# One transpose for the last 16 columns of four batches, and copies inside SBUF for the row tiles

## The chip, the cores and the metric

The kernel runs on one core of a Trainium2 chip. The time is device microseconds for one execution. The core's engines are named as the profile names them: PE is TensorE (PEld its weight loads), DVE is VectorE, ACT is ScalarE, POOL is GpSimd, and SP is SyncE, which here only issues DMAs.

## What is computed

The input x has 32 batches of 128 tokens by 144 columns, with one condition vector of 144 per batch. Four layers follow one another: a transformer layer with normalised q and k (L0), a rotation of x inside a subspace of 64 columns (L1), a plain transformer layer (L2), and a transformer layer with four experts in place of its MLP (L3). All is float32. Cut to what the change touches:

```python
def _modulate(x, shift, scale):
    return x * (1.0 + scale) + shift

ada = jax.nn.silu(c) @ W_ada + b_ada
shift_msa, scale_msa, gate_msa, shift_mlp, scale_mlp, gate_mlp = jnp.split(ada, 6, axis=-1)
h = _modulate(_layernorm(x), shift_msa, scale_msa)
x = x + gate_msa * _attention(h, W_qkv, b_qkv, W_proj, b_proj)
h = _modulate(_layernorm(x), shift_mlp, scale_mlp)
mlp = jax.nn.gelu(h @ W_fc1 + b_fc1, approximate=True) @ W_fc2 + b_fc2
x = x + gate_mlp * mlp
```

L0 and L3 have the same frame; L3's MLP is `hmid = gelu(xf @ w1[e] + b1[e])` for four experts, weighted by a softmax over the two largest of four gate logits `xf @ w_gate`. The rotation is

```python
U, _ = jnp.linalg.qr(P)
R = _rotation(cond, W, b)                  # expm of a skew matrix, 64 x 64 per batch
z = jnp.einsum('btn,nd->btd', x, U)
x_rot = x + jnp.einsum('btd,nd->btn', jnp.einsum('btd,bde->bte', z, R) - z, U)
```

## The kernel before

x stays in SBUF with tokens on the partitions. A product that contracts over the 144 columns needs them on the partitions, of which there are 128. So each normalised batch h is split into a main part of 128 columns and a rest of 16, both transposed on PE: `hM` (128 x 128 per batch) and `hR` (the 16 columns; a 17th row of ones carries the bias of the weights). Each product is then a main product over 128 rows and a rest product added to it.

The rest product needs only 17 rows, fewer than a fourth of PE's 128. So the 16 columns are laid down four times before the transpose, at columns 0, 32, 64 and 96 of the tile `xr`; its transpose then holds four copies at partitions 0, 32, 64 and 96, in four *row tiles* of 32. Rest products of four different outputs use one row tile each (`rows4(m)`, 32 rows) and run on PE side by side, with the rest weights `wqkR`, `wvR`, `w1R` laid out to match. L0's q, k and v are formed differently (`by_token0`), with one rest product over all 128 rows, in which only 17 are filled.

The batches go in eight groups of four (G = 4). What a group goes through for one normalisation, of kind "a" (before attention) or "m" (before the MLP):

- `ln_stats` (L616): mean and variance on DVE, then on POOL the normalised main part `xh` (L636) and the four copies of the rest in `xr` (L638), per batch. `xr` comes from a ring of 7 zeroed tiles.
- `ln_T` (L645): per batch two transposes on PE, `xh` (L655) and `xr` (L656), into one PSUM bank, and two ACT instructions (L658) that scale and shift them, with `modM` and `modR`, into the group's `hM` and `hR`. `modR` holds shift and scale of the 16 columns four times over.
- The readers: `qk_chunks` (four products of 512 columns for q and k of a group: four main products, then four rest products, both in the helper `both`, L668), `values` by `by_token` (two batches at a time), `fc1` (three row tiles, up to three outputs at a time; for most calls the rest products stand first and the main products a gap later), and `gate_logits` (L1026), which multiplies the four batches into four column tiles.

The rotation has its own transposes: `rotate_T` (L988) turns main and rest of the four batches, eight transposes, and `rotate_in` (L1005) multiplies by U's main part `uM` and rest `uR`.

The order of all work is written out by hand. Time goes in *ticks*, one per batch and layer; in each tick the scores of one batch (two calls, n = 0 and 1) alternate with the weighing of another, and between them are named *gaps* ("a", "e", "t", "stats", "b0", "b", "den", "pre1", "c", "y1" ... "z", "d"), into which `put` places the other work. Each engine carries out its instructions in that order. The second and third attention layers start at ticks 35 and 67. With t0 the first tick of a group, in the second layer:

- the "a" statistics of batch i stand in tick t0 - 6 + i, its `ln_T` in gap "b" of the tick after (group 0: t0 - 4 + i // 2);
- `qk_chunks` in gap "c" of t0 - 2; the values at t0 and t0 + 1;
- the "m" statistics at t0 + 3 + i and its `ln_T` in gap "d" of the same tick; `fc1` at t0 + 8 and t0 + 9;
- the rotation of the next layer's input, `rotate_T`, `rotate_in` and `rotate`, in the ticks t0 - 8 and t0 - 7.

In the third layer `ln_T` of "a" stands in gap "d" of its statistics' own tick, and the gates at t0 + 7 are followed by `moe1` from t0 + 8 on. Gap "d" stands at a tick's end from tick 35 on, "b" and "c" in its middle. SP's queue holds the loads of x and the weights, of each group's gates (`load_gates`, L305), and the stores of the output (L1138).

## Time and profile before

| | us |
|---|---|
| median of 3 runs | 1312.52 (1311.24 to 1313.37) |
| profiled execution, its time | 1303.81 |
| profiled execution, span of its instructions | 1302.1 |

Groups of instructions that the change touches, by line, in the profiled execution:

| line | what | count | mean ns |
|---|---|---|---|
| L655 PE | transposes of xh, "a" and "m" | 96 + 96 | 286, 275 |
| L656 PE | transposes of xr, "a" and "m" | 96 + 96 | 281, 273 |
| L658 ACT | hR out of PSUM, "a" and "m" | 96 + 96 | 462, 461 |
| L638 POOL | xr, 128x64 | 187 | 420 |
| L668 PE | rest products of qk, 32x512 | 128 | 640 |
| L668 PE | rest products of fc1, 32x512 | 448 | 619, 613 |
| L1000 PE | transposes of the rotation's rest | 32 | 277 |
| L305 SP | loads of the gates | 48 | |

A matmul's duration is modelled, and matmuls overlap: the next begins long before the one before it ends, so that what an instruction takes of PE's time is read from the distance between starts. Most matmuls here count twice, as float32 takes two passes; a transpose counts once. L668 is a helper's line, so its groups are told apart by their tiles.

### The profile page before, as it was taken

The page shows a single profiled execution, that of the slowest core. Times are in us where ns is not written, and L with a number is a line of the kernel's source. Part 1 is how long each engine was busy: PE and PEld are TensorE (multiplying, and loading weights), DVE is VectorE, ACT ScalarE, POOL GpSimd, SP SyncE. Part 2 cuts the span into 40 slices and gives each one's busy share as a digit, 9 for nine tenths or more (in the row PEclk, how much of TensorE's full clock was granted, in tenths as well). Part 3 has the DMA queues.
Part 4 walks back from the last instruction along what each step waited for, and adds up shares of the span by engine and source line. Part 5 has one row for each costly group of instructions (what it writes and reads, how often), then busy time and mean ns, then how long its engine had stood idle before and what let it go on. Part 6 is the DMA issues. An engine that isn't in the chain of part 4 may idle for free.

```text
span 1302.1 us, 35663 instructions
## 1 busy us (share of the span) xinstructions
PE 1259.5 (97%) x14180; PEld 920.3 (71%) x14180; DVE 807.7 (62%) x2534; ACT 833.4 (64%) x1832; POOL 690.4 (53%) x1667
## 2 busy tenths in 40 slices
PE   6989898999999999999999999999999999999998
PEld 4678676786776667767777766767676767677666
DVE  5698888876774457667666666646464646455343
ACT  3568677678767566777767777665656555555431
POOL 5667777665753345445445554746464636361610
PEclk9999999999999999999999999999999999999999
DMA  8200000000003000000110000200000000000000
GB/s 234 62 2 21 20 7 15 20 3 22 20 2 134 19 11 21 11 20 20 37 29 20 20 11 11 76 11 19 11 20 11 19 11 19 11 19 2 19 10 10
DMA packets 21720, 34.43 MB, mean 26 GB/s; under 512 B 2353, under 2 KB 12497, under 8 KB 21297
## 3 DMA queue, kind: packets, MB, share of 16 engines
q1 hardware_dynamic: 20896, 31.70, 8.1%
q8 instruction: 114, 1.87, 0.6%
q10 hardware_dynamic: 656, 0.42, 0.2%
q14 instruction: 54, 0.43, 0.1%
HBM read 29.65 MB, written 2.47 MB: 25 GB/s over the span
## 4 chain that ended last, share of the span: by engine, by line
PE 71%; DVE 3%; ACT 1%; issue 0%; POOL 0%; DVEq 0%; POOLq 0%
PE ps_h L668 19%; PE ps_f L1118 10%; PE ps_s L856 7%; PE ps_qk L668 6%; PE ps_w L856 6%; PE ps_o L883 5%; PE ps_f L977 5%; PE ps_pj L947 3%; PE ps_v L668 2%; PE ps_f L1123 1%; PE ps_o L815 1%; DVE nm L861 1%; PE ps_z L1009 1%; PE ps_hT_m L656 1%; PE ps_cw L1106 1%; PE ps_hT_m L655 1%
## 5 line engine op out<-in xcount | busy, mean ns | idle before, releaser
L861 DVE TENSOR_REDUCE nm<-ps_s 128x4 f32<-128x512 f32 x384 | 246.3, 682 | 89.4 <-PE ps_w L856 67.8
L868 ACT ACTIVATE pr<-ps_w 128x512 f32<-128x512 f32 x384 | 208.6, 595 | 106.1 <-PE ps_w L856 104.6
L856 PE MATMUL ps_s<-kT,qT 32*128 32x256 f32 x1536 | 228.4, 404 | 0.7 <-ACT kT L791 0.6
L856 PE MATMUL ps_w<-q,kT 32*128 32x128 f32 x3072 | 229.0, 283 | 0.0
L856 PEld LDWEIGHTS ps_w<-q,kT 32*128 32x128 f32 x3072 | 194.2, 187 | 9.8 <-issue 6.2
L971 ACT ACTIVATE hid<-ps_h 128x512 f32<-128x512 f32 (+1 forms) x224 | 120.0, 591 | 100.1 <-PE ps_h L668 99.6
L856 PEld LDWEIGHTS ps_s<-kT,qT 32*128 32x128 f32 x1536 | 134.5, 184 | 29.6 <-issue 8.6
L668 PE MATMUL ps_h<-hM_m,mlps 128*128 128x512 f32 x304 | 144.0, 607 | 0.0
L1127 DVE SCALAR_TENSOR_TENSOR acc<-ps_f,cw,acc 128x144 f32<-128x144 f32 x128 | 46.7, 366 | 149.5 <-PE ps_f L1118 74.3
L933 POOL TENSOR_TENSOR x_sb<-x_sb,res_a 128x144 f32<-128x144 f32 x96 | 47.1, 490 | 146.7 <-DVE res_a L936 145.9
L883 PE MATMUL ps_o<-pr,vaug 128*32 128x128 f32 x3072 | 104.2, 276 | 0.3 <-issue 0.3
L883 PEld LDWEIGHTS ps_o<-pr,vaug 128*32 128x32 f32 x3072 | 78.1, 109 | 33.4 <-PE ps_w L856 18.9
L668 PEld LDWEIGHTS ps_h<-hM_m,mlps 128*128 128x128 f32 x304 | 53.3, 189 | 67.5 <-issue 66.6
L734 POOL TENSOR_SCALAR kT<-kT,cst 128x512 f32<-128x512 f32 x40 | 62.4, 1564 | 61.5 <-ACT kT L721 60.5
L977 PE MATMUL ps_f<-mlps,hid 128*128 128x144 f32 x640 | 93.5, 293 | 0.0
L977 PEld LDWEIGHTS ps_f<-mlps,hid 128*128 128x128 f32 x640 | 82.4, 191 | 7.8 <-issue 3.2
L868 ACT ACT_TABLE_LOAD x57 | 73.1, 1283 | 6.5 <-PE ps_w L856 5.7
L629 POOL TENSOR_SCALAR rs_m_a<-mv_m_a 128x2 f32<-128x2 f32 x81 | 15.6, 193 | 114.4 <-DVE mv_m_a L627 86.1
L968 ACT ACT_TABLE_LOAD x58 | 74.4, 1283 | 1.0
L658 ACT ACTIVATE hM_m<-ps_hT_m,modM 128x128 f32<-128x128 f32 x96 | 44.7, 465 | 45.5 <-PE ps_hT_m L656 45.4
L1118 PEld LDWEIGHTS ps_f<-pair,hid 128*128 128x128 f32 x512 | 66.9, 190 | 8.4 <-issue 7.7
L1118 PEld LDWEIGHTS ps_f<-mlps,hid 128*128 128x128 f32 x512 | 66.7, 190 | 8.1 <-issue 7.2
(328 smaller groups left out, 2918.5 us busy)
## 6 DMA issues: line engine op xcount, KB each, us to landing
gates<-gates SPq DMA_DIRECT2D x48, 288.0 KB, 3.5
x_sb<-in_x SPq DMA_DIRECT2D x8, 288.0 KB, 9.2
out_x<-x_sb SPq DMA_DIRECT2D x7, 288.0 KB, 2.5
mlps<-in_L_mlp SPq DMA_DIRECT2D x2, 1000.0 KB, 6.2
pair<-in_L_mlp SPq DMA_DIRECT2D x1, 1800.0 KB, 11.8
mlps<-in_L_mlp SPq DMA_DIRECT2D x1, 1800.0 KB, 8.2
pow<-in_W SPq DMA_DIRECT2D x4, 320.0 KB, 6.5
mlps<-in_L_wmod SPq DMA_DIRECT2D x4, 290.0 KB, 4.8
```

Of the source, the lines that this page charges most:

```text
L668: nc.tensor.matmul(ps, x, y, start=k == 0, stop=k == 1)
L734: eng.tensor_scalar(o, k, m, None, ALU.mult)
L856: nc.tensor.matmul(o, x, y, start=True, stop=True)
L861: nc.vector.tensor_reduce(nmv[:, at0 : at0 + 2, ONE : ONE + 2], view.rearrange("p (r t k) -> p r t k", t=2, k=T), AX.X, ALU.max, negate=True,)
L868: nc.scalar.activation(pr[:, 4 * e : 4 * e + 4, :].rearrange("p s q -> p (s q)"), view, AF.Exp, scale=SCALE,)
L883: nc.tensor.matmul(po[rows4(j), t, :], v[:, 4 * j + 2 * t + r, :], prs[j // 2][:, 4 * (j % 2) + 2 * r + t, :], start=r == 0, stop=r == 1,)
L933: nc.gpsimd.tensor_tensor(x_sb[:, b, :], x_sb[:, b, :], t, ALU.add)
L968: nc.scalar.activation(t, half, AF.Gelu_apprx_tanh)
L971: nc.scalar.activation(hid[:n, i], ps[:n], AF.Gelu_apprx_tanh)
L977: nc.tensor.matmul(ps, hid[:, at0, i, :], w2[:, m, :], start=m == 0, stop=m == NFC - 1)
L1118: nc.tensor.matmul(ps[:, 0, :], hid[:, at0 + m, i, :], w2[:, at0 + m, :], start=m == 0, stop=m == 3)
L1127: nc.vector.scalar_tensor_tensor(acc, ps[:, 0, :], w, acc, ALU.mult, ALU.add)
```

## The change

All the rest transposes of a group, apart from L0's "a", become one. `xr` is now written once per batch, 16 columns at column 32 i of a tile shared by the group's four batches (`take_xg`, a ring of four; `take_xr` keeps three tiles for L0's "a"). When the last batch's `ln_T` comes, one transpose turns the shared tile, and one ACT instruction scales and shifts it into `hG`, in which partition 32 i + c is column c of batch i. Its shift and scale are `modG`, made of `modR` by four POOL copies.

Readers that need one batch in one row tile now take `hG` itself: `by_token` uses row tile i0 + i for batch i0 + i, and `gate_logits` uses all 128 rows with the rest weights on the diagonal (batch i's rows 32 i, and its own 32 columns of a 128 x 128 weight tile). Readers that need all four batches in every row tile (`qk_chunks`, `fc1`) still read `hR`, which is now filled by DMAs on SP's queue: for each row tile m, and each batch j, a copy of `hG`'s 32 rows of batch j, 32 x 128 float32 (16 KB), 16 copies for "a" and 12 for "m". In the second layer the last batch's "a" `ln_T` moves from gap "b" of a tick to gap "d" of the tick before. In the rotation one transpose replaces the four of the rest, and the rest product becomes four products over 128 rows, each with a U that is filled in one batch's rows alone. `modR` of the later layers moves to a pool that is given back after the preparation.

```diff
-    take_xr = ring([128, 128], "xr", 7, zeros)
+    take_xr = ring([128, 128], "xr", 3, zeros)
+    take_xg = ring([128, 128], "xg", 4, zeros)
...
+        mg = const.tile([128, 4, NG], F32, name=f"modG{n}")
+        for i in range(G):
+            nc.gpsimd.tensor_copy(
+                mg[rows4(i)], mr[rows4(i)].rearrange("p k (g i) -> p k g i", i=G)[:, :, :, i]
+            )
...
-        nc.vector.tensor_copy(uR, ps[:, 1, :])
+        for i in range(G):
+            nc.vector.tensor_copy(uR[rows4(i), i, :], ps[rows4(i), 1, :])
...
-            xr = take_xr()
-            nc.gpsimd.tensor_scalar(
-                xr.rearrange("p (k c) -> p k c", k=4)[:, :, :CR],
-                x_sb[:, b, CM:].unsqueeze(1).to_broadcast([128, 4, CR]),
-                minus, r, ALU.add, ALU.mult,
-            )
-            st[s][f"xh_{kind}"], st[s][f"xr_{kind}"] = xh, xr
+            if (layer, kind) == (0, "a"):
+                xr = st[s]["xr_a"] = take_xr()
+                to = xr[:, :CR]
+            else:
+                if i == 0:
+                    gr[g][f"xr_{kind}"] = take_xg()
+                to = gr[g][f"xr_{kind}"][:, 32 * i : 32 * i + CR]
+            nc.gpsimd.tensor_scalar(to, x_sb[:, b, CM:], minus, r, ALU.add, ALU.mult)
...
-        nc.tensor.transpose(ps[:, 1, :], st[s].pop(f"xr_{kind}"), ident)
-        for k, m in (("hM", modM[layer]), ("hR", modR[layer])):
+        todo = [(gr[g][f"hM_{kind}"][:, i, :], modM[layer], b)]
+        if single:
+            nc.tensor.transpose(ps[:, 1, :], st[s].pop("xr_a"), ident)
+            todo.append((gr[g]["hR_a"][:, i, :], modR[layer], b))
+        elif i == G - 1:
+            nc.tensor.transpose(ps[:, 1, :], gr[g].pop(f"xr_{kind}"), ident)
+            hG = work.tile([128, T], F32, tag=f"hG_{kind}", name=f"hG_{kind}_{s}", bufs=1)
+            gr[g][f"hG_{kind}"] = hG
+            todo.append((hG, modG[layer], g[1]))
+        for k, (to, m, c) in enumerate(todo):
             nc.scalar.activation(
-                gr[g][f"{k}_{kind}"][:, i, :], ps[:, k == "hR", :], AF.Identity,
-                bias=m[:, sh, b : b + 1], scale=m[:, sc, b : b + 1],
+                to, ps[:, k, :], AF.Identity,
+                bias=m[:, sh, c : c + 1], scale=m[:, sc, c : c + 1],
             )
+        if not single and i == G - 1:
+            hR = work.tile([128, G, T], F32, tag=f"hR_{kind}", name=f"hR_{kind}_{s}")
+            gr[g][f"hR_{kind}"] = hR
+            for m in range(4 if kind == "a" else 3):
+                for j in range(G):
+                    nc.sync.dma_start(hR[rows4(m), j, :], hG[rows4(j)])
...
-            [(ps, hR[rows4(i), i0 + i, :], wR[rows4(i)]) for i, ps in enumerate(pss)],
+            [(ps, hG[rows4(i0 + i)], wR[rows4(i0 + i)]) for i, ps in enumerate(pss)],
...
-        for i in range(G):
-            xr = take_xr()
-            nc.gpsimd.tensor_copy(xr[:, :CR], x_sb[:, n * G + i, CM:])
-            nc.tensor.transpose(ps[:, i, :], xr, ident)
+        xr = take_xg()
+        nc.gpsimd.tensor_copy(
+            xr.rearrange("p (i c) -> p i c", i=G)[:, :, :CR], x_sb[:, n * G : n * G + G, CM:]
+        )
+        nc.tensor.transpose(ps, xr, ident)
...
+        for i in (0, 2, 1, 3):
+            h = i // 2
+            nc.tensor.matmul(
+                ps[h * D : (h + 1) * D, i % 2, :], uR[:, i, :], xR, start=False, stop=i % 2 == 1
+            )
...
+        for i in range(G):
+            nc.tensor.matmul(
+                ps[rows4(i)], L3.wgateR[:, 32 * i : 32 * i + 32], hG, start=False, stop=True
+            )
...
-                    put(*((at_a, "d") if at_a != t0 + i - ahead else (at_a + 1, "b")), ln_T, s, "a")
+                    end = at_a != t0 + i - ahead or (layer, i) == (1, G - 1)
+                    put(*((at_a, "d") if end else (at_a + 1, "b")), ln_T, s, "a")
...
+    rest = np.zeros((128, 128), w.dtype)
+    for i in range(G):
+        rest[32 * i : 32 * i + CR, 32 * i : 32 * i + 32] = w[CM:]
+    arrays["L3_wgateR"] = rest
```

More of the change, by code (lines that the diff above doesn't have):

```diff
@@ L260, in tile_kernel @@
     gates = dram.tile([3, 2, B * C], F32, name="gates")
-    modM, modR = [], []
+    modM, modR, modG = [], [], []
     def modulations(n):
@@ L265, in modulations @@
         mm = const.tile([128, 4, B], F32, name=f"modM{n}")
-        mr = const.tile([128, 4, B], F32, name=f"modR{n}")
+        mr = (pp if n else const).tile([128, 4, B], F32, name=f"modR{n}")
         ps = bank([128, 8, B], f"ps_mod{n}")
@@ L281, in modulations @@
         nc.vector.tensor_scalar_add(mr[:, 2:, :], ps[:, 6:8, :], 1.0)
+        mg = const.tile([128, 4, NG], F32, name=f"modG{n}")
[3 more added lines that the diff above has]
+            )
         modM.append(mm)
         modR.append(mr)
+        modG.append(mg)
     def layer_gates(n):
@@ L312, in tile_kernel @@
     uM = const.tile([128, D], F32, name="uM")
-    uR = const.tile([128, D], F32, name="uR")
+    uR = const.tile([128, G, D], F32, name="uR")
+    nc.gpsimd.memset(uR, 0.0)
     rotU = const.tile([128, NB2, C], F32, name="rotU")
@@ L387, in prep_qr @@
         nc.vector.memset(ur, 0.0)
-        nc.vector.tensor_copy(ur[:, :CR], uT[:D, CM:])
+        nc.vector.tensor_copy(
+            ur.rearrange("p (i c) -> p i c", i=G)[:, :, :CR],
+            uT[:D, CM:].unsqueeze(1).to_broadcast([D, G, CR]),
+        )
         yield
@@ L632, in ln_stats @@
         for k, (s, kind) in enumerate(pairs):
-            b = of(s)[1]
+            layer, b, g, i = of(s)
             minus, r = rs[:, 1, k : k + 1], rs[:, 0, k : k + 1]
@@ L636, in ln_stats @@
             nc.gpsimd.tensor_scalar(xh, x_sb[:, b, :CM], minus, r, ALU.add, ALU.mult)
-            xr = take_xr()
-            nc.gpsimd.tensor_scalar(
-                xr.rearrange("p (k c) -> p k c", k=4)[:, :, :CR],
-                x_sb[:, b, CM:].unsqueeze(1).to_broadcast([128, 4, CR]),
-                minus, r, ALU.add, ALU.mult,
-            )
-            st[s][f"xh_{kind}"], st[s][f"xr_{kind}"] = xh, xr
+            if (layer, kind) == (0, "a"):
[6 more added lines that the diff above has]
+            nc.gpsimd.tensor_scalar(to, x_sb[:, b, CM:], minus, r, ALU.add, ALU.mult)
+            st[s][f"xh_{kind}"] = xh
     def ln_T(s, kind):
         layer, b, g, i = of(s)
+        single = (layer, kind) == (0, "a")
         if i == 0:
-            for k in ("hM", "hR"):
+            for k in ("hM", "hR") if single else ("hM",):
                 gr[g][f"{k}_{kind}"] = work.tile(
@@ L672, in by_token @@
     def by_token(g, kind, i0, n, w, wR, name, rest_first=False):
-        hM, hR = gr[g][f"hM_{kind}"], gr[g][f"hR_{kind}"]
+        hM, hG = gr[g][f"hM_{kind}"], gr[g][f"hG_{kind}"]
         pss = [bank([128, w.shape[1]], f"{name}_{i0 + i}") for i in range(n)]
@@ L990, in rotate_T @@
         xM = work.tile([128, G, T], F32, tag="xM", name=f"xM_{n}", bufs=1)
-        xR = work.tile([128, G, T], F32, tag="xR", name=f"xR_{n}", bufs=1)
+        xR = work.tile([128, T], F32, tag="xR", name=f"xR_{n}", bufs=1)
         ps = bank([128, G, T], f"ps_xT_{n}")
@@ L995, in rotate_T @@
         nc.scalar.copy(xM, ps)
-        ps = bank([128, G, T], f"ps_xR_{n}")
-        for i in range(G):
-            xr = take_xr()
-            nc.gpsimd.tensor_copy(xr[:, :CR], x_sb[:, n * G + i, CM:])
-            nc.tensor.transpose(ps[:, i, :], xr, ident)
+        ps = bank([128, T], f"ps_xR_{n}")
+        xr = take_xg()
[3 more added lines that the diff above has]
+        nc.tensor.transpose(ps, xr, ident)
         nc.scalar.copy(xR, ps)
@@ L1006, in rotate_in @@
         ps = bank([128, 2, T], f"ps_z_{n}")
-        for u, x in ((uM, xM), (uR, xR)):
-            for h in range(2):
-                nc.tensor.matmul(
-                    ps[h * D : (h + 1) * D], u, x[:, 2 * h : 2 * h + 2, :],
-                    start=u is uM, stop=u is uR,
-                )
+        for h in range(2):
+            nc.tensor.matmul(
+                ps[h * D : (h + 1) * D], uM, xM[:, 2 * h : 2 * h + 2, :], start=True, stop=False
+            )
[3 more added lines that the diff above has]
+                ps[h * D : (h + 1) * D, i % 2, :], uR[:, i, :], xR, start=False, stop=i % 2 == 1
+            )
         zT = work.tile([128, 8, T], F32, tag="pr", name=f"zT_{n}", bufs=4)[:, :2, :]
@@ L1028, in gate_logits @@
         gr[g]["lg"] = lg = small.tile([128, G, E], F32, tag="lg", name=f"lg_{g[1]}", bufs=2)
-        hM, hR = gr[g]["hM_m"], gr[g]["hR_m"]
+        hM, hG = gr[g]["hM_m"], gr[g]["hG_m"]
         ps = bank([128, T], f"ps_g_{g[1]}")
-        for w, h in ((L3.wgate, hM), (L3.wgateR, hR)):
-            for i in range(G):
-                nc.tensor.matmul(ps[rows4(i)], w, h[:, i, :], start=h is hM, stop=h is hR)
+        for i in range(G):
+            nc.tensor.matmul(ps[rows4(i)], L3.wgate, hM[:, i, :], start=True, stop=False)
+        for i in range(G):
+            nc.tensor.matmul(
+                ps[rows4(i)], L3.wgateR[:, 32 * i : 32 * i + 32], hG, start=False, stop=True
+            )
         lgT = late.tile([128, T], F32, tag="lgT", name=f"lgT_{g[1]}")
@@ L1540 @@
     main_and_rest("L3_wgate", w, np.zeros(32, w.dtype), 1)
+    rest = np.zeros((128, 128), w.dtype)
+    for i in range(G):
+        rest[32 * i : 32 * i + CR, 32 * i : 32 * i + 32] = w[CM:]
+    arrays["L3_wgateR"] = rest
     for name, (wn, bn) in _MOD.items():
```

## The prediction, made before the changed kernel was run

> **What bounds the kernel now.** I read the page first (its engine row and the chain that ended last), then the busy time by stage, then the stretches of the timeline in which the edited lines stand.

> ```profile
> span 1302.1 us, 35663 instructions
> PE 1259.5 (97%) x14180; PEld 920.3 (71%) x14180; DVE 807.7 (62%) x2534; ACT 833.4 (64%) x1832; POOL 690.4 (53%) x1667
> ...
> PE 71%; DVE 3%; ACT 1%; issue 0%; POOL 0%; DVEq 0%; POOLq 0%
> ...
> 420.00:700.00 280.00, 278.77 (x3219) 197.83 (x3211) 172.01 (x493) 196.48 (x387) 131.36 (x297) 1.00 0.07 21
> ...
> 820.00:1215.00 395.00, 394.39 (x3786) 279.52 (x3781) 205.52 (x620) 231.49 (x438) 197.15 (x397) 1.00 0.06 17
> ```

> The last two rows are two stages: the window, its length, then what PE, PEld, DVE, ACT and POOL were busy. PE is busy 97% of the span, and in the second layer's stage (420 to 700 us) and the third's (820 to 1215) all but 1.2 and 0.6 us; the chain runs over PE. ACT, DVE and POOL have a third or more to spare. So a matmul taken from PE's stream counts in full, a wait put into it counts in full, and work saved on ACT and POOL counts for nothing by itself. All sums are against this execution (span 1302.1 us, 1303.8 with its edges); it lies 8.7 us under the median of the runs, 1312.5, and I carry differences over one to one.

> **What goes.** Three transposes a group fall away in each normalisation that is not the first layer's "a": first layer "m", second and third "a" and "m", 5 x 8 = 40 groups, 120 transposes. Each of the 8 rotations loses 3 more: 144.

> ```profile
> 571.86 0.27 PE L815 MATMUL ps_o<-cst,nm 128*128 128x128 f32 x1
> 571.97 0.27 PE L655 MATMUL ps_hT_m<-cst,xh_m 128*128 128x128 f32 x1
> 572.08 0.27 PE L656 MATMUL ps_hT_m<-cst,xr 128*128 128x128 f32 x1
> 572.28 0.76 PE L1022 MATMUL ps_d<-rotU,zT 64*128 64x144 f32 x8
> ```

> The rows last 0.27 us but start 0.11 us apart: they are pipelined, and what one is worth is the spacing. 144 x 0.109 (the finer start times) = **-15.7 us**. The 0.27 would say 39 us and is too much. 120 ACT copies (462 ns, 0.34 apart) also go; ACT is not the bound, so 0. POOL's copy of 64 columns (420 ns) shrinks to 16 (the 128x16 copy of L999 takes 195): 0 likewise. In the rotation, two products of 256 columns by two passes become four of 128 by two: as many columns, 0.

> **What is added: copies.** After the group's last batch ACT writes hG, and the SP queue issues 16 copies of 32x128 ("a") or 12 ("m") into hR. Two readers use hG directly and need no copy: the value products and the gates. The others are the rest products of qk and of fc1 (the helper of L668). No copy of this kind stands in the trace; the nearest are these.

> ```profile
> 394.32 0.42 SPq L106 DMA_DIRECT2D L_wproj<-in_L_wproj  x1
> 394.78 0.43 SPq L174 DMA_DIRECT2D mlps<-in_L_mlp  x1
> 395.26 0.43 SPq L106 DMA_DIRECT2D L_wgate<-in_L_wgate  x1
> 395.73 0.43 SPq L106 DMA_DIRECT2D L_wgateR<-in_L_wgateR  x1
> ...
> DMA to landing us min/median/max: 1.4/1.5/5.4
> ```

> Issues in a burst start 0.465 us apart, whatever their size. The last line is of the gates' 32-row tile gsb written out of SBUF, 18 KB, the shape closest to a copy: 1.5 us to landing. Its two issues stand 0.36 apart (the first after a pause is shorter). So the sixteenth starts 0.36 + 14 x 0.465 = 6.9 us after the first and lands 1.5 later; with 0.03 for SP to wake (gsb's own delay) and 0.1 for the last waits on PE, **8.5 us from hG's end**. Bounds: 15 x 0.36 + 1.4 = 6.8; and the wider spacing of 0.49 at 631.7 us with the 1.9 us of the condition load (0.79 to 2.64): 9.5. Twelve "m" copies take 6.6 by the same sum.

> Where is hG's end, and when does PE want the copies? Second layer, a group in the middle:

> ```profile
> 572.88 0.45 ACT L658 ACTIVATE hM_m<-ps_hT_m,modM 128x128 f32<-128x128 f32 x1
> 573.22 0.45 ACT L658 ACTIVATE hR_m<-ps_hT_m,modR 128x128 f32<-128x128 f32 x1
> ...
> 577.14 0.27 PE L655 MATMUL ps_hT_a<-cst,xh_a 128*128 128x128 f32 x1
> ...
> 578.56 3.70 PE L668 MATMUL ps_qk<-hM_a,L_wqk 128*128 128x512 f32 x8
> 582.19 1.14 PE L668 MATMUL ps_qk<-hR_a,L_wqkR 32*128 32x512 f32 x8
> ```

> The change moves the last batch's transposes from gap b of tick t0-2 (577.14) to gap d of the tick before, beside the "m" transposes that ACT empties from 572.88. There hR_m goes unless it is the fourth batch's, so hM_a starts at 573.22, hG at 573.56 and ends at 574.02. Of the move: POOL has xh_a ready at 569.9, two us before gap d, so PE does not wait there; behind it stand the rotation's ps_d, the projection and the next scores, 0.11 us later for one more transpose, while 0.25 goes at 577.14. PE reaches the rest products at 582.05, 8.03 us after hG. The fourth row tile needs copies 13 to 16: **late by 0.5 us**. The same reading of the other groups:
> - second layer, groups 3 to 6: 8.03 each, 4 x 0.5 = 2.0; groups 1 and 2: 8.4, 0.1 each; group 7 (hG at 689.0, rest at 696.44): 7.4, 1.1; group 0, whose last batch moves from 429.75 to beside 425.61: 6.7, 1.8
> - third layer, groups 0 to 2, in the short ticks before 820 us: (hG 725.4, rest 733.0) 7.6, 3 x 1.0 = 3.0
> - third layer, groups 3 to 7: rest 864.17, hG 846.9, 17 us, none
> - all "m" groups: the shortest stretch is hG 586 to fc1 597.2, 11 us against 6.6, none.

> Sum **+8.1 us**; by the bounds 0 and 18. A late copy holds PE's queue: behind the rest products wait the transpose of nm (583.26), fc2 and the scores, so nothing covers it.

> [...]

> SP's queue otherwise: gates loads, the loads of L3's weights and the output stand in program order, and each waits only for work at least a tick older than the copies behind it; they issue up to 7.5 us later than now, with two ticks or more to their first use. Landing order on 8 semaphores: copy k waits for copy k-8, 3.7 us older, no delay.

> **What is added: waits on PE.** A rest product now waits for four copies, each with its own semaphore. A weight load carries one wait; the others become EVENT_SEMAPHORE instructions, two waits in each.

> ```profile
> L668 PEldq EVENT_SEMAPHORE  x5: 51/51/51, 429.0 to 429.4; - x5
> ```

> Five in a row start 0.106 us apart, satisfied or not. By the instruction order of the changed kernel a qk group gets 8 of them (0.85 us) and the first fc1 call of a group 6 more than now (0.64 us). At qk they are read while the main products run (3.6 us), so 0. At fc1 the rest stands first, behind the scores, where the sequencer is 0.7 us ahead of the array (the wait of 596.44 belongs to the load of 597.15): 0.64 just fits, with less room where two were there already. I take 0.1 for 24 groups, **+2.4 us**; bounds 0 (room enough) and 24 x 0.64 = 15.

> **Edits at nothing.** modG costs POOL 4 copies of about 0.2 us three times, hidden under PE's preparation; without that cover 0.8 at the start, which I keep as a bound beside 0.3 saved there by shorter xr copies. Four uR copies in place of one, the rings, modR's pool, the gates' weights on the diagonal (as many products): 0.

> **Sum.** -15.7 + 8.1 + 2.4 = -5.2: span 1296.9, time **1307**. Extremes: -16 (1296.5) and -15.7 + 18 + 15 + 0.8 = +18 (1330.6).

> **Rivals.**
> - *All copies in time.* Landing 1.4 or less, or issues at 0.36, leave at most group 0 waiting; with 1 us of waits, 1312.5 - 14.7 = 1298. For it: the issue of a small tile was once 0.31 us, and a copy that stays in SBUF may land sooner than gsb's. Against: issues that follow another took 0.42 to 0.43 in every burst. 0.17.
> - *Late copies decide, slower.* In the qk rest products of 11 groups; from a need of 9.3 us on (0.8 more than my sum) the 12 groups lose 9 to 10 us more and the gain is gone; at 10.5 us the copies cost 8.1 + 12 x 2 = 32, so 1331. For it: the first two writes of gsb landed only after 4.8 and 5.4 us, with other traffic about, and loads from HBM here take 1.9 to 6; against: in the stages in question the DMA engines are busy 0.07 of the time. 0.24.
> - *The waits' own instructions show in full.* Slower: 15 instead of 2.4 at fc1, 1320; decides above 0.3 us a group. For it: leads as short as 0.03 to 0.2 us before fc1 between 711 and 795 us. Against: 0.7 in the steady groups. 0.13.
> - *My forecast*, partly late copies, 1303 to 1313: 0.46.
> - That the transposes do not go is excluded by the instruction order: 144 fewer products on PE.

> **How the numbers follow.** The measurement tells 0.2% (2.6 us) from no change. Forecast case: two thirds of it below 1309.9 (0.31), the rest within (0.13) or a little slower (0.02). First rival faster (0.17); late copies slower (0.21) or even (0.03); wait instructions slower (0.12) or even (0.01). Faster 0.48, same 0.17, slower 0.35. The time is the forecast's, 1307. Its own range is 1301 to 1313; the range for 8 in 10 takes half of the first rival and the lower half of the slower ones: 1299 to 1326.

> **What would show it.** Right: PE's rows start-to-start without the 144 transposes; in the second layer the group's period falls from 38.9 us by 0.97 less about 0.5; rest products of qk that wait for a DMA by 0.5 us in groups 3 to 6 and by 1 us at 733, none after 820; SP rows of hR 0.465 apart, landing in 1.5. Wrong: landings over 2.3 us or spacings over 0.52 (slower), no wait at qk at all (1298), gaps ahead of fc1's rest products with no wait named (the wait instructions), or PE idle for POOL in gap d at 572 us.

## The result and the profile after

The changed kernel is slower: 1375.91 us median (4 runs, 1364.68 to 1378.36) against 1311.88 for the kernel before (4 runs, 1302.98 to 1313.37), a ratio of 1.048, 95% interval 1.0436 to 1.0524. The profiled execution took 1374.31 us, its span is 1372.6.

The head of the page and its chain of waits, changed kernel:

```profile
span 1372.6 us, 36289 instructions
PE 1307.4 (95%) x14068; PEld 943.0 (69%) x14068; DVE 806.4 (59%) x2537; ACT 791.4 (58%) x1712; POOL 682.8 (50%) x1656
...
PE 58%; SPq 8%; DVE 3%; ACT 3%; DMA 2%; issue 1%; POOL 0%; ACTq 0%; DVEq 0%
```

PE has 112 products fewer (144 transposes less, 8 x 4 more in the rotation), as announced, and yet it is busy 48 us longer. The chain, which ran over PE for 71%, now runs over SP's queue for 8% and over DMAs for 2%. The two stages shown of before (window, its length, busy time of PE, PEld, DVE, ACT and POOL, then PE's granted clock):

```profile
420.00:700.00 280.00, 267.43 (x2876) 185.04 (x2874) 154.51 (x450) 162.98 (x314) 113.87 (x253) 0.96 0.09 25
820.00:1215.00 395.00, 388.46 (x3727) 270.94 (x3728) 203.94 (x608) 219.24 (x407) 197.42 (x394) 0.98 0.10 28
```

PE stands 12.6 us of the first stage where it stood 1.2. Two things are new: idle time, and a clock under 1.00. What PE waited for between 420 and 1215 us (total, times, longest):

```profile
PE ps_qk L697 <- DMA hR_a<-hG_a: 20.4, 18, 1.5
PE ps_o L844 <- DVE nm L890: 2.1, 5, 0.9
PE ps_h L697 <- DMA hR_m<-hG_m: 0.9, 1, 0.9
```

And the row of the "a" copies in the view of the tile hR_a (duration of an issue in ns: least, median, longest):

```profile
L690 SPq DMA_DIRECT2D hR_a<-hG_a x256: 507/588/1728, 440.3 to 1189.4; - x128
```

The stall is where the prediction put it, but larger. One group of the second layer, SP's issues first, then PE:

```profile
560.08 11.15 SPq L690 DMA_DIRECT2D hR_a<-hG_a  x16
571.33 0.53 SPq L312 DMA_DIRECT2D gates<-gates  x1
```

```profile
568.36 1.13 PE L697 MATMUL ps_qk<-hR_a,L_wqkR 32*128 32x512 f32 x4
570.04 1.09 PE L697 MATMUL ps_qk<-hR_a,L_wqkR 32*128 32x512 f32 x2 [0.56 <-DMA hR_a<-hG_a]
572.49 2.07 PE L697 MATMUL ps_qk<-hR_a,L_wqkR 32*128 32x512 f32 x2 [1.36 <-DMA hR_a<-hG_a]
574.49 0.47 PE L844 MATMUL ps_o<-cst,nm 128*128 128x128 f32 x1
```

hG ends at 560.05. The sixteen issues begin 0.63 us apart, and the last copy lands 12.4 us after hG. PE reaches the rest products after 8.3 us and needs 6.13 us from there to the next instruction instead of 1.07 before. Before, the four rest products ran side by side; now they run as their copies land, two, then one and one (each counts twice), so that the view names only part of the stretch as idle. The last one takes 2.07 us instead of 1.09: it runs at half clock. The clock over that stretch, by windows of 5 us (columns as above):

```profile
565.00:570.00 5.00, 4.48 (x12) 1.46 (x11) 1.79 (x4) 1.53 (x4) 1.74 (x4) 1.00 0.09 21
570.00:575.00 5.00, 3.60 (x7) 1.30 (x8) 0.00 (x0) 1.58 (x4) 0.00 (x0) 0.69 0.20 72
575.00:580.00 5.00, 5.00 (x48) 4.59 (x51) 1.17 (x4) 0.99 (x3) 1.31 (x3) 0.62 0.01 3
580.00:585.00 5.00, 5.00 (x79) 4.50 (x72) 4.49 (x13) 4.12 (x8) 4.62 (x7) 1.00 0.11 25
```

After the stall PE is fully busy from 575 to 580 us and runs at 0.62 of its speed. So this stall cost twice: while PE waited, and again after it.

By group (times from the trace; "stretch" is from the first qk rest product to the next other product on PE, 1.07 us in every group of before; the half-clock stretches are those of the trace's clock record):

| group | hG's end to rest products | first issue to last landing | stretch | half clock from, for |
|---|---|---|---|---|
| 2nd layer, 0 | 6.5 | 11.2 | 6.10 | 452.5, 3.4 |
| 1 | 8.3 | 11.2 | 4.92 | 486.6, 6.8 |
| 2 | 8.6 | 11.6 | 4.32 | none |
| 3 | 8.3 | 12.4 | 6.13 | 571.9, 6.8 |
| 4 | 8.3 | 11.2 | 4.05 | none |
| 5 | 8.3 | 12.1 | 4.93 | 660.7, 3.4 |
| 6 | 8.3 | 11.8 | 4.79 | 705.1, 3.4 |
| 7 | 7.5 | 11.2 | 4.89 | 746.0, 3.4 |
| 3rd layer, 0 | 7.4 | 11.6 | 5.78 | 787.0, 6.8 |
| 1 | 7.4 | 12.0 | 6.38 | 831.4, 6.8 |
| 2 | 7.4 | 11.6 | 5.45 | 875.7, 3.4 |
| 3 to 7 | 17.3 | 11.2 to 13.0 | 1.07 | none |

A further half-clock stretch, 3.4 us from 892.8, follows the one wait of 0.88 us for an "m" copy, at 890.5.

**Where the time went.** From the first group's qk products in the second layer to the last group's in the third, 692.1 us became 750.4: +58.2. The eleven stretches add 57.7 - 11 x 1.07 = 46.0, the "m" wait 0.9, the ten half-clock stretches (47.8 us at half speed) 23.9. The version below in which no copy is late takes 684.0 for the same part, so the rest of the change brings -8.1. The sum, 46.0 + 0.9 + 23.9 - 8.1, is 62.7, which is 4.5 too much: 7.3 us of the half clock lie inside the stretches and are counted there already, which takes 3.6 off; 0.9 is left over. Ahead of that part the changed execution is 12.6 us later than the profiled one before; the second profile of the kernel before, at the end of the experiments, speaks to that.

### The profile page after: what moved, and what is told of

Its sections match the earlier page's. It is cut to its first block, busy times and chain, and to the rows that moved or that the text cites. A ratio compares the mean times of both kernels' runs of the same rounds, so it can differ in the third digit from the quotient of the medians.

```text
span 1372.6 us, 36289 instructions
## 1 busy us (share of the span) xinstructions
PE 1307.4 (95%) x14068; PEld 943.0 (69%) x14068; DVE 806.4 (59%) x2537; ACT 791.4 (58%) x1712; POOL 682.8 (50%) x1656
## 4 chain that ended last, share of the span: by engine, by line
PE 58%; SPq 8%; DVE 3%; ACT 3%; DMA 2%; issue 1%; POOL 0%; ACTq 0%; DVEq 0%
PE ps_h L697 17%; PE ps_f L1154 9%; SPq L690 8%; PE ps_s L885 5%; PE ps_w L885 5%; PE ps_o L912 4%; PE ps_f L1006 4%; PE ps_qk L697 3%; PE ps_v L697 2%; PE ps_pj L976 2%; DMA hR_a<-hG_a 1%; PE ps_f L1159 1%; DVE nm L890 1%; ACT pr L897 1%; PE ps_o L844 1%
## 5 line engine op out<-in xcount | busy, mean ns | idle before, releaser
L885 PE MATMUL ps_s<-kT,qT 32*128 32x256 f32 x1536 | 234.0, 412 | 0.6 <-ACT kT L820 0.6
L885 PE MATMUL ps_w<-q,kT 32*128 32x128 f32 x3072 | 233.8, 286 | 0.1
L885 PEld LDWEIGHTS ps_w<-q,kT 32*128 32x128 f32 x3072 | 198.2, 190 | 11.6 <-issue 7.3
L885 PEld LDWEIGHTS ps_s<-kT,qT 32*128 32x128 f32 x1536 | 138.1, 190 | 30.0 <-issue 11.8
L962 POOL TENSOR_TENSOR x_sb<-x_sb,res_a 128x144 f32<-128x144 f32 x96 | 46.9, 489 | 160.5 <-DVE res_a L965 159.7
L1006 PE MATMUL ps_f<-mlps,hid 128*128 128x144 f32 x640 | 102.8, 312 | 0.0
L912 PEld LDWEIGHTS ps_o<-pr,vaug 128*32 128x32 f32 x3072 | 79.3, 111 | 33.2 <-PE ps_w L885 13.6
L1006 PEld LDWEIGHTS ps_f<-mlps,hid 128*128 128x128 f32 x640 | 91.1, 207 | 7.8 <-issue 3.8
L962 POOL TENSOR_TENSOR x_sb<-x_sb,res_m 128x144 f32<-128x144 f32 x64 | 32.5, 512 | 124.4 <-DVE res_m L965 124.3
L849 DVE TENSOR_TENSOR q<-qT,ps_o 128x256 f32<-128x256 f32 x62 | 25.9, 418 | 95.0 <-PE ps_o L844 95.0
```

The costliest lines, as they stand in the source:

```text
L885: nc.tensor.matmul(o, x, y, start=True, stop=True)
L912: nc.tensor.matmul(po[rows4(j), t, :], v[:, 4 * j + 2 * t + r, :], prs[j // 2][:, 4 * (j % 2) + 2 * r + t, :], start=r == 0, stop=r == 1,)
L962: nc.gpsimd.tensor_tensor(x_sb[:, b, :], x_sb[:, b, :], t, ALU.add)
L1006: nc.tensor.matmul(ps, hid[:, at0, i, :], w2[:, m, :], start=m == 0, stop=m == NFC - 1)
```

## Experiments

The theory: the copies come late because sixteen small DMAs are issued one after another on one queue, 0.63 us each, and most such stalls of PE are followed by half clock. Against it stood: that copies inside SBUF are slow or disturb PE whatever their number; that the wait instructions cost the time; and, for the start, that the edits there are to blame.

**Half the copies.** Only row tiles 0 and 1 are filled for "a"; the third and fourth rest product of qk use them again.

```diff
-            for m in range(4 if kind == "a" else 3):
+            for m in range(2 if kind == "a" else 3):
...
-            [(ps, p.wqkR[rows4(m), cols[m]], hR[rows4(m)]) for m, ps in enumerate(pss)],
+            [(ps, p.wqkR[rows4(m % 2), cols[m]], hR[rows4(m % 2)]) for m, ps in enumerate(pss)],
```

> The changed kernel with a copies for row tiles 0 and 1 alone (8 instead of 16); the third and fourth rest product of qk use row tiles 0 and 1 again, where wqkR holds the same weights, so two run side by side instead of four: 2.14 us instead of 1.07 for each of 16 groups, +17 us on PE. Theory A (the number of issues on one queue decides): 0.56 + 6 x 0.633 + 1.8 = 6.2 us from hG, less than the 7.4 to 8.0 that PE leaves, so no DMA wait at qk and no half-clock stretch after it: 1376 - 46 - 22 + 17 = 1325, give or take 13 for the start. Rival B (copies inside SBUF are late or slow PE whatever their number): waits at qk stay over 20 us, time over 1360.

Measured: 1314.85 us, ratio to before 1.0034 (1.0002 to 1.0066). The stretch is 1.92 us in all sixteen groups, no DMA wait at qk is left, and the two stages are at full clock:

```profile
420.00:700.00 280.00, 278.43 (x3206) 195.89 (x3203) 170.97 (x495) 180.48 (x347) 127.70 (x281) 1.00 0.10 29
820.00:1215.00 395.00, 394.20 (x3765) 275.38 (x3766) 202.28 (x607) 221.14 (x409) 199.91 (x403) 1.00 0.08 24
```

The copies take the same way, inside SBUF, at the same price each (0.588 us median in both); only their number is halved. That removes some 60 us, although the pairs cost PE 16 x 0.85 = 13.6. So it is not the kind of copy; whether the number of issues or the halved traffic did it, the next experiment tells.

**Fewer and larger DMAs, by way of DRAM.**

```diff
+            hD = dram.tile([128, T], F32, name=f"hD_{kind}_{s}")
+            nc.sync.dma_start(hD, hG)
             for m in range(4 if kind == "a" else 3):
-                for j in range(G):
-                    nc.sync.dma_start(hR[rows4(m), j, :], hG[rows4(j)])
+                nc.sync.dma_start(hR[rows4(m)], hD.rearrange("(j p) t -> p j t", j=G))
```

> The changed kernel, but hG is written once to a 64 KB DRAM tile, and each row tile of hR is read back by one DMA of 32 partitions x 4 x 512 B: 5 (a) or 4 (m) DMAs a group instead of 16 or 12, one wait a rest product instead of four. Theory A (number of issues in the burst): 2.0 us for the write, 0.36 + 2 x 0.465 for the issues, 2 to 2.6 for the last landing, some 6 to 6.5 us from hG, under the 8.0 that PE leaves: DMA waits at qk under 5 us in all instead of 20 named and 46 of stretch; third-layer period 65.57 - 0.65 = 64.9 us (65.2 in the changed kernel) if the wait instructions are what fc1 lost; time 1312 - 15.7 + 3 = 1299, or 1313 if the start stays late. Rival B (traffic): four times the bytes through HBM, so no better than the changed kernel's 1376.

Measured: 1296.81 us, ratio to before 0.9922 (0.9888 to 0.9956). It beats both kernels, the one before by 0.8%. Its SP and PE at the same group:

```profile
572.28 0.34 SPq L689 DMA_DIRECT2D hD_a<-hG_a  x1
575.64 1.74 SPq L691 DMA_DIRECT2D hR_a<-hD_a  x4
577.48 0.38 SPq L312 DMA_DIRECT2D gates<-gates  x1
```

```profile
576.92 3.70 PE L698 MATMUL ps_qk<-hM_a,L_wqk 128*128 128x512 f32 x8
580.56 1.14 PE L698 MATMUL ps_qk<-hR_a,L_wqkR 32*128 32x512 f32 x8
581.63 0.33 PE L845 MATMUL ps_o<-cst,nm 128*128 128x128 f32 x1
```

Here the write took 3.3 us to land (1.5 is the median; the 2.0 expected was an estimate that no run had shown), and still the last read landed 6.6 us after hG, 1.7 ahead of PE. Issues that read from DRAM start 0.47 us apart, those that write to it take 0.34: the 0.465 that the prediction took from loads holds for loads. The traffic theory falls: every copied byte now passes through DRAM and no wait at qk is left. The number of issues is the cause. One number missed: the third layer's period is 65.19 us, as in the changed kernel (65.20), not 64.9. This version has 87 wait instructions on PE at the line of these products, the changed kernel 287, so the extra wait instructions cost nothing that shows.

**Two queues.** The odd row tiles' copies are issued from ScalarE's queue.

```diff
-                    nc.sync.dma_start(hR[rows4(m), j, :], hG[rows4(j)])
+                    q = nc.scalar if m % 2 else nc.sync
+                    q.dma_start(hR[rows4(m), j, :], hG[rows4(j)])
```

> The changed kernel with the copies of the odd row tiles issued from ScalarE's queue. Theory A with issues that run side by side: 8 issues a queue, 0.56 + 6 x 0.633 + 1.8 = 6.2 us after hG, no wait at qk, but ScalarE is held some 5 us a burst, and exp results and PSUM drains behind it come late: PE waits on ACT of up to 3 us a burst in 28 bursts; time between 1300 and 1360. If both queues share one descriptor generator: spacing over both queues stays 0.63 us, last landing 11 us after hG, the qk waits stay, and ScalarE's hold comes on top: 1380 to 1420.

Measured: 1405.61 us, ratio 1.0699 (1.0644 to 1.0753). One burst of 8 and 8 issues in the view of hR_a (columns as above):

```profile
L691 SPq DMA_DIRECT2D hR_a<-hG_a x8: 513/596/732, 937.8 to 942.4; - x8
L691 ACTq DMA_DIRECT2D hR_a<-hG_a x8: 522/620/870, 937.8 to 942.7; - x8
```

What PE waited for from 420 us on:

```profile
PE ps_qk L698 <- ACT pr L898: 29.0, 10, 4.0
PE ps_h L698 <- ACT hM_a L681: 6.5, 4, 1.6
```

The queues issue side by side, each at its old pace, and in this burst the last copy lands 6.7 us after hG (6.0 to 9.8 over the sixteen "a" bursts, as far as the trace has their landings). So it is the queue that is slow, not something that both share. But ScalarE's own work stands behind its issues, and PE now waits for ScalarE: 29 us for exp results (`pr`) alone, and six of these ten waits led to half clock too. The range expected for this case, up to 1360, was too low; the time lies in the range given for a generator that both queues share, but the sign of that, 0.63 us between issues over both queues, is absent.

**Twice the copies where none was late** (third layer, groups 3 to 7).

```diff
                     nc.sync.dma_start(hR[rows4(m), j, :], hG[rows4(j)])
+                    if layer == 2 and kind == "a" and g[1] > 2:
+                        nc.sync.dma_start(hR[rows4(m), j, :], hG[rows4(j)])
```

> The changed kernel with every a copy of the third layer's groups 3 to 7 issued twice (32 issues a burst instead of 16). These groups had no wait: the last copy landed some 12 us after hG and PE came after 17.3. Theory A: 32 issues end 20 us after hG and land at 22: PE stands 4 to 5 us in the qk rest products of these 5 groups, 23 us in all, and after most of the five the clock is half for 3.4 or 6.8 us (1.7 or 3.4 us lost each): some 30 us over the changed kernel, 1405, and half-clock stretches now near 940, 1005, 1070, 1140 and 1210 us. Rival B (traffic as such): no new wait at qk, some us at most.

Measured: 1494.84 us in one run. The stretches of these groups grew from 1.07 to 24.6 to 26.1 us, not by 4 to 5: the second copy of each pair writes where the first does and waits until that has landed, so a pair takes 2.37 us and the last landing came 40 us after hG. The size was foreseen wrongly, the sign and the place rightly. After each of the five, and of the eleven stalls before, the clock is halved (16 of 16). One of the five, in windows:

```profile
923.00:928.00 5.00, 5.00 (x32) 2.35 (x25) 1.29 (x2) 3.89 (x6) 0.00 (x0) 1.00 0.06 13
928.00:933.00 5.00, 1.58 (x4) 0.29 (x2) 0.00 (x0) 1.17 (x2) 0.00 (x0) 1.00 0.07 16
933.00:957.00 24.00, 9.09 (x26) 5.96 (x26) 1.69 (x4) 2.06 (x5) 3.12 (x2) 0.50 0.09 22
957.00:962.00 5.00, 5.00 (x69) 3.02 (x68) 2.38 (x7) 3.15 (x7) 1.83 (x5) 1.00 0.09 20
```

PE's work thins out from 928.5 on (one product in the next 12 us), the clock falls at 933.0 and comes back some 5 us after the last rest product.

**Fewer rows in each copy**, 20 instead of 32; the rest products run over 20 rows too.

```diff
-                    nc.sync.dma_start(hR[rows4(m), j, :], hG[rows4(j)])
+                    nc.sync.dma_start(hR[32 * m : 32 * m + 20, j, :], hG[32 * j : 32 * j + 20])
...
```

> The changed kernel with 20 of the 32 rows copied, and the rest products over 20 rows (the other 12 meet weights that are zero). If an issue's price goes by its rows: spacing about 0.40 instead of 0.633 us, last landing near 8 us after hG, the stretch of the qk rest products near 1.1 to 1.6 us instead of 4.1 to 6.4, time 1320 to 1330. If the price is one of the instruction (its kind, from SBUF to SBUF): spacing 0.60 to 0.63, all as in the changed kernel, 1365 to 1390.

Measured: 1401.09 us in one run, outside both expectations: an issue became dearer. The copies up to 1215 us in the view of hR_a:

```profile
L690 SPq DMA_DIRECT2D hR_a<-hG_a x252: 706/707/1600, 435.9 to 1214.4; - x126
```

One burst on the timeline:

```profile
613.63 12.03 SPq L690 DMA_DIRECT2D hR_a<-hG_a  x16
```

The issues are 0.75 us apart instead of 0.63, the stretches 6.8 to 8.8 us instead of 4.1 to 6.4, and all eleven are followed by half clock (13.7 us after the first). So fewer bytes and fewer rows did not lower the price of an issue here: its median went from 0.588 to 0.707 us. Why it rose is not shown.

**The "m" half alone.** Attention's normalisation as before; 96 of the 144 transposes go, 288 of the 544 copies stay. POOL writes attention's 16 columns once instead of four times here, so that in the second and third layer three of the four row tiles hold no remainder.

```diff
-            if (layer, kind) == (0, "a"):
+            if kind == "a":
...
-        single = (layer, kind) == (0, "a")
+        single = kind == "a"
...
```

> The change for the second normalisation (m) and for the rotation alone; the attention normalisation (a) of the second and third layer as before, with four transposes and four scalar-engine copies a group. 96 of the 144 transposes go, 288 of the 544 copies stay. Theory A (PE stands in the qk rest products because sixteen issues 0.633 us apart plus 1.8 us to landing end 11 to 12 us after hG, when PE is there after 8; each such stand is followed by a stretch at half clock): no DMA wait at qk, no half-clock stretch between 430 and 880 us; -10.5 for the transposes, +0.28 x 24 = +6.7 at the first rest products of fc1, so 4 us under the kernel before, about 1308, if the start of the program is as before. Rival B (DMA traffic as such, or the wait instructions, slows PE wherever the copies are): about half of the +63 us stays, 1340. Rival C (the late full clock at the start comes from the edits to the start that this kernel keeps: modG, shorter xr): +14, 1322, with full clock first near 67 us instead of 27.

Measured: 1309.62 us, ratio 0.9976 (0.9950 to 1.0002). No DMA wait at qk. The copies of "m" are late twice in all (between 420 and 1215 us):

```profile
PE ps_h L697 <- DMA hR_m<-hG_m: 1.7, 2, 1.1
```

The longer one, at 827 us, is followed by the only half-clock stretch between 225 us and the program's end (3.4 us from 829.2), and that group took 60.5 us instead of 57.1. Second-layer period: 38.31 us against 38.90 before, with six transposes a group fewer. Rival B (1340) is wrong, and so is the time of the start's rival (1322), though this profile too has full clock late, first at 57.8 us.

**The transposes' own price.** The DRAM version with the 120 transposes of the normalisations put back, of the identity, their results unread.

```diff
-        elif i == G - 1:
+        elif i < G - 1:
+            nc.tensor.transpose(ps[:, 1, :], ident, ident)
+        else:
             nc.tensor.transpose(ps[:, 1, :], gr[g].pop(f"xr_{kind}"), ident)
```

> The version with one write to DRAM and 3 or 4 reads, with the 120 transposes of the normalisations put back, of the identity into the half bank that they used to fill, their results unread: it prices the transposes alone. At 0.109 us each on PE, as the prediction had it: +13 us, third-layer period 65.20 + 6 x 0.109 = 65.85. If part of each was hidden (the period of the third layer fell by 0.38 instead of 0.65): +7.5, period 65.57. Nothing else differs.

Measured: 1309.71 us, ratio 1.0005 (0.9977 to 1.0034), against 0.9922 without them. Third-layer period 65.52 against 65.19, second-layer 38.69 against 38.36: in both, six transposes are worth 0.33 us, 0.055 each instead of 0.109 (the medians differ by more, with an interval of several us; the periods of the two profiles of before agree to 0.05). This is a mean: with the "m" half alone, which keeps three more transposes a group, the second layer's period was no longer than the DRAM version's, 38.31 against 38.36. Comparing starts product by product shows how, here in the third layer: each transpose taken out moves the products behind it 0.109 us ahead, and in the next score group that stands before fc1 the second pair's products (`ps_w`) start 0.27 us after the first (`ps_s`) instead of 0.16, so that 0.1 is given back there. What holds `ps_w` back then is not settled.

**The kernel before, again.**

> The kernel before once more, for a second profile of it. If the late start of the changed kernel (full clock at 67 us instead of 27) is chance: full clock first at another time than 26.9 us, anywhere between 25 and 70, with the start that much longer or shorter (0.35 us a us), and the third-layer period 65.57 again. If it is the edits: 27 again, within 3.

Measured: 1307.24 us. Full clock first at 41.4 us, not 26.9, and the second layer's first qk products 3.8 us later; periods 38.89 and 65.52 as before. Over the profiles, first full clock and the time of these products: before 26.9 and 430.7, before again 41.4 and 434.5, changed kernel 66.8 and 443.3, the kernel with twice the copies (the same program up to there) 42.1 and 429.9, the one with half of them (the same again) 27.2 (but half again from 30.6 to 64.8) and 441.1, the "m" half 57.8 and 439.1, DRAM version 41.8 and 431.7. The same program differs by 13.4 us, so an execution's chance is enough for the 12.6 us at the start. That the edits there cost nothing is not shown by this: both profiles of before are among the early ones. One caution on reading it: the windows view prints 1.00 until the clock's first record; that PE is slow there is seen from durations, such as these transposes of the changed kernel (0.27 us at full clock):

```profile
66.16 0.42 PE L670 MATMUL ps_hT_a<-cst,xh_a 128*128 128x128 f32 x1
66.37 0.42 PE L673 MATMUL ps_hT_a<-cst,xr 128*128 128x128 f32 x1
```

## Why the prediction was wrong

- **PE as the bound, every wait in full:** right. The whole loss is waits of PE and what follows them.
- **When PE wants the copies:** right. 8.0 us from hG was read, 8.3 measured; 6.7, 7.4 and 7.6 for the special groups, 6.5, 7.5 and 7.4 measured; no wait at qk in the third layer's groups 3 to 7.
- **When the copies are there (8.5 us):** the step that failed. "Issues in a burst start 0.465 us apart, whatever their size" was read from loads out of DRAM and carried over to copies with both ends in SBUF, which the trace of before did not hold. Measured: 0.63 apart, 1.8 us to landing, 11.2 us from hG, and up to 12.4 in bursts with one long issue. The upper bound, 9.5, came from the same kind of row and so bounded nothing. With these two figures the prediction's own sum gives 11.4 us, and by its own margins the copies then cost 40 us instead of 8; 46 was measured.
- **What a stall costs:** missing. The prediction counted a late copy once, as PE's waiting. Ten stretches at half clock added 23.9 us, 20.3 of it outside the waits, and no rival had them, though the kernel before shows halved clock too, in its first 215 us.
- **The transposes (-15.7):** too large. The spacing of two transposes, 0.109 us, is not what one is worth where the scores behind it give part back: 0.055 measured for those of the normalisations, and -8.1 over the two layers, the rotation's included, instead of -13.
- **The wait instructions (+2.4, and the rival of 1320):** nothing shows. The reading behind it, that waits start 0.106 us apart "satisfied or not", does not hold either: for the five behind it, 429.0 to 429.4, every awaited semaphore had been raised before (the last at 428.7), and in the group shown above, waits for copies that had not landed start 0.60 and 0.65 us apart, with the copies.
- **ACT, POOL and the rotation at nothing:** nothing in these runs speaks against it.
- **The rivals:** "late copies decide, slower" was the mechanism and had 0.24. Its price, 1331 at a need of 10.5 us, was short of the need, of the clock and of what the transposes give back (and it counts 12 groups where the prediction's list has 11).

## What to carry to other kernels

Price a DMA by a row with the same two ends: here a copy inside SBUF cost its queue 0.63 us and a load 0.47, and with sixteen in a burst the difference decided; where a copy is wanted several times, a few larger DMAs, even by way of DRAM, can beat many small ones (here 5 or 4 a group with 1296.81 us, 16 or 12 with 1375.91). A wait on a TensorE that was hardly ever idle can cost more than its length (here 46.9 us of waits, and 20.3 more at half clock): look at the granted clock after it. And price a removed instruction by putting it back in the version that works, not by its spacing alone (here 0.055 us against 0.109).
